# A convolution block on one core: the ternary weights' pieces halved in width and given two buffers, the second weights' extremes moved into the main loop, zeros stored ahead of the weights

## Chip, core and metric

The kernel runs on one core of one Trainium2 chip. The metric is the device time of one execution in microseconds. Before the change three runs took 2253.93, 2255.93 and 2258.55 us; their median, 2255.93 us, is the time before.

## What is computed

The input is `x` of shape (8, 256, 56, 56) in fp32. Two layers follow each other, each with a skip connection.

```
# layer 0: an involution of the group-normed input
g = groupnorm(x, 32 groups)
ker = w_span @ (w_reduce @ g + b_reduce) + b_span        # 16 groups of 7*7 weights for each pixel
x = x + sum over the 7*7 neighbours of ker * neighbour(g)

# layer 1: two 3*3 convolutions with ternary weights
def ternary(w):                       # over the whole tensor (256, 256, 3, 3)
    tw = w - mean(w)
    mx, mn = max(tw), min(tw)
    lo, hi = mn + (mx - mn) / 3, mx - (mx - mn) / 3
    return where(tw < lo, -1, where(tw > hi, 1, 0))
def conv(v, w): return conv3x3(v, ternary(w)) + centre tap once more
o1 = relu(batchnorm(conv(groupnorm(x), w1)))
o2 = batchnorm(conv(o1, w2))
x = x + relu(o1 + o2)
```

The change concerns the weights `w1` and `w2` of layer 1. Each has 256 x 256 x 9 numbers, held as 128 partitions of 4608. To make a weight ternary, the kernel first needs its mean, its largest and its smallest element, then one pass over it with the two thresholds. That pass also forms six "planes" from the three taps of each filter row (sums and differences of the taps), since the convolution is done in a Winograd manner over the rows. The planes go to a DRAM scratch tensor `wqd`, from which the convolution stage loads them much later.

## The kernel before

Four stages follow each other. The start loads the first image, takes its group-norm statistics, and makes the first of the matrices described next. The main loop does layer 0. Then come the two convolutions, and a last stage that adds everything up and stores the output.

**Main loop.** An image is cut into four quarters of 64 channels (the two halves of the picture fill the 128 partitions). A quarter is worked in ten rows of tiles, so there are 8 x 4 x 10 = 320 rows. For each quarter a matrix `a` is made from the reduced image `kr` in 14 units (`generate`, line 761). In a unit, TensorE writes `pg` (line 782), and ScalarE (line 786) and VectorE (line 791) move it with its bias into `a`. TensorE's `pg` has two PSUM buffers, so a unit waits until the one before the last is emptied. A row (`apply_row`, line 801) multiplies `a` with `q`, the patches of the input: four sevenths of a `q` come by DMA from the DRAM scratch `xtd` (line 742), the rest from TensorE transposes of `xe` (line 749, copied at 752). Its result `pa` goes through ScalarE (`inv`, line 827) and VectorE (line 828) to GpSimd (called POOL in the profile), which adds it to `x` (line 831). The rows of a quarter interleave with the units of the next quarter, and with the statistics, the group-norm parameters and the reductions `pk` (line 651) of the next image.

`xtd` is filled by `prep` (line 695): POOL writes a normed strip into the single buffer `xn` (line 674), TensorE transposes it (line 717), ScalarE copies it out (line 720), SP stores it (line 708). The borders of `xtd` must be zero. They are stored once in the start, at line 637, as sixteen DMAs whose source is `xn`, which then still holds zeros. POOL therefore cannot write its first strip before these sixteen have landed.

**Order of the work.** Almost all DMAs are issued by SP, one after the other as the text has them; an issue waits for its data, for its target buffer, and for one of eight semaphores to come free from an earlier DMA. Some stores are put into a list `tasks` and issued by `transfer`, two at the start of each row. Within a row the tile framework's order is the order of the text; `pin` (line 864) ties the last instruction of each row to the first of the next on every engine.

**Extremes, before.** Line 627 takes the buffer `wf` and the four DMAs of line 631 fill it with all of `w1` and `w2`, ahead of the zeros. `extremes` (line 195) is a generator: six times a maximum and a minimum on VectorE (lines 208 and 209, 768 elements each) and a sum on ScalarE (line 210); then the partial results are joined, TensorE sums and transposes them across partitions (lines 222, 223 and 230), and some tiny VectorE instructions give the mean and the two thresholds. Line 900 chains the twelve steps of both weights and then both endings; three steps are taken after each third of the first image's reduction (line 906), the others one after each unit of the first matrix (line 914).

**Pieces, before.** `quantize` (line 248) makes a weight ternary in 16 pieces of 96 output columns (`QN`), 288 elements a partition. A piece has one buffer, `piece`. Line 257 loads it; then, a yield apart, come lines 261 and 262 (two comparisons), 264 to 277, 279 to 281, 283 and 284. The store (line 287, six planes of 96 columns) is put into `tasks`. One piece takes seven rows, and the next piece begins when the store has been issued. Both weights' pieces run one after the other from row 8 on (`QUANT_AT`): 32 pieces in 224 rows, some five and a half images; line 984 takes one step at the end of each row.

Of the kernel before, what the change touches and what calls it, by code (L numbers as in the profile page):

```python
# [2 lines left out]

# [5 lines left out]
F32 = mybir.dt.float32  # L9
F32R = mybir.dt.float32r  # L10
AF = mybir.ActivationFunctionType
ALU = mybir.AluOpType
# [5 lines left out]
P = 128  # L18
B, C, H, W = 8, 256, 56, 56
HW = H * W  # L20
CT = C // P
# [37 lines left out]
A_COLS = (NT * NP + NE * PX) * GQ  # L59
# [19 lines left out]

QN, QJ = 96, 3 * C // 96
QS = WT
SLOT = (0, 2, 3, 4, 5, 1)
QM = 6


@with_exitstack
def involution_tri_block_kernel(
# [3 lines left out]
    nc = tc.nc  # L93
# [11 lines left out]
    wq_d = [dram.tile([P, QS * CT * 3 * C], F32, tag=f"wqd{i}", name=f"wqd{i}") for i in range(2)]  # L105
# [84 lines left out]
        return sc, bi  # L190

    def piece_of(pool, name):
        return pool.tile([P, (4 + QS) * QN], F32, tag="piece", name=f"piece_{name}")

    def extremes(w, cols, pool, transposer, psum_tile, name):
# [8 lines left out]
        s, mx, mn = col(QM), col(QM), col(QM)  # L204
        f = nf // QM
        for j in range(QM):
            v = w[:, j * f:(j + 1) * f]
            nc.vector.tensor_reduce(mx[:, j:j + 1], v, AX.X, ALU.max)
            nc.vector.tensor_reduce(mn[:, j:j + 1], v, AX.X, ALU.min)
            nc.scalar.activation(v, v, AF.Identity, accum_out=s[:, j:j + 1])  # L210
            yield
        sums, ends = col(), col(2)
        nc.vector.tensor_reduce(sums, s, AX.X, ALU.add)
        nc.vector.tensor_reduce(ends[:, 0:1], mx, AX.X, ALU.max)
        nc.vector.tensor_reduce(ends[:, 1:2], mn, AX.X, ALU.min)
        nc.vector.tensor_scalar(ends[:, 1:2], ends[:, 1:2], -1.0, None, ALU.mult)
        v = piece_of(pool, name)
        nc.vector.memset(v[:, :P], 1.0)
        yield

        ps = psum_tile(f"ends_{name}")
        nc.tensor.matmul(ps[:, P:P + 1], v[:, :P], sums, start=True, stop=True)
        nc.tensor.transpose(ps[:2, :P], ends, transposer)
        mean, top = cols[:, 0:1], col()
# [3 lines left out]
        yield  # L228
        ps = psum_tile(f"all_{name}")
        nc.tensor.transpose(ps[:, :2], v[:2, P:2 * P], transposer[:2, :2])  # L230
        ex = col(2)
# [6 lines left out]
        d, q0, r, th = (col() for _ in range(4))  # L238
# [9 lines left out]
    def quantize(dst, w_dram, cols, pool, tasks, name):  # L248


        mean, lo, hi = (cols[:, k:k + 1] for k in range(3))
        for t in range(CT):
            for j in range(QJ):
                v = piece_of(pool, name)
                w, u = v[:, :3 * QN], v[:, 3 * QN:]
                o = (t * QJ + j) * 3 * QN
                nc.sync.dma_start(w, w_dram[:, o:o + 3 * QN])
                yield
                yield
                g = u[:, :3 * QN]  # L260
                nc.vector.tensor_scalar(g, w, mean, hi, ALU.subtract, ALU.is_gt)
                nc.vector.tensor_scalar(w, w, mean, lo, ALU.subtract, ALU.is_lt)
                yield
                nc.vector.tensor_tensor(g, g, w, ALU.subtract)

                def part(x, k):
                    return x[:, k * QN:(k + 1) * QN]


                c0, c1 = max(C, j * QN) - j * QN, min(2 * C, (j + 1) * QN) - j * QN  # L270
                if c0 < c1:
                    g1 = part(u, 0)[:, c0:c1]
                    nc.vector.tensor_scalar(g1, g1, 2.0, None, ALU.mult)

                e, f = part(w, 0), part(w, 1)
                g1, g0, g2 = (part(u, k) for k in range(3))
                nc.vector.tensor_tensor(e, g0, g2, ALU.add)
                yield
                nc.vector.scalar_tensor_tensor(f, g2, 4.0, g0, ALU.mult, ALU.add)
                nc.vector.tensor_tensor(part(u, 3), e, g1, ALU.add)  # L280
                nc.vector.tensor_tensor(part(u, 4), e, g1, ALU.subtract)
                yield
                nc.vector.scalar_tensor_tensor(part(u, 5), g1, 2.0, f, ALU.mult, ALU.add)
                nc.vector.scalar_tensor_tensor(part(u, 6), g1, -2.0, f, ALU.mult, ALU.add)

                def store(u=u[:, QN:], o=t * 3 * C + j * QN):
                    nc.sync.dma_start(
                        bass.AP(dst[:].tensor, dst[:].offset + o,
                                [[QS * CT * 3 * C, P], [CT * 3 * C, QS], [1, QN]]), u)

                tasks.append(store)
                yield
                yield

    def weights(i, k):

# [221 lines left out]
    with ExitStack() as ph1:  # L518
# [19 lines left out]
        apool1 = ph1.enter_context(tc.tile_pool(name="apool1", bufs=1))  # L538
# [71 lines left out]
        ident_sb = fixed([P, P], "ident_sb", ident)  # L610
# [11 lines left out]
        xe = [fixed([P, NX, HQ, QX], f"xe{i}") for i in range(2)]  # L622
        for v in xe:
            nc.gpsimd.memset(v, 0.0)

        nf = CT * 9 * C
        wf = apool1.tile([P, A_COLS], F32, tag="a1", name="wf")
        for i, v in enumerate((w1, w2)):
            for j in range(2):
                o = j * nf // 2  # L630
                nc.sync.dma_start(wf[:, i * nf + o:i * nf + o + nf // 2], v[:, o:o + nf // 2])
        zero = xn.rearrange("p k r x -> p (k r x)")

        for d in (d for ds in xt_d for d in ds):
            for r0, n in ((0, PAD), (PAD + HH, HQ - PAD - HH)):
                e = n * QX * RP // P
                nc.sync.dma_start(
                    bass.AP(d[:].tensor, d[:].offset + r0 * QX * RP, [[e, P], [1, e]]), zero[:, :e])

        def reduce(b, py):  # L640

# [254 lines left out]
        thresholds = [pieces.tile([P, 32], F32, tag=f"cols{i}", name=f"cols{i}") for i in range(2)]  # L896
        ext = [extremes(wf[:, i * nf:(i + 1) * nf], thresholds[i], pieces, ident_sb, ps_one, f"w{i}")
               for i in range(2)]
# [34 lines left out]
        for k in rows[:QLEAD]:  # L933
            transpose_q(*k)
        pin()
        norm = iter(())
        quant = chain(*(quantize(wq_d[i], v, thresholds[i], pieces, tasks, f"w{i + 1}")
                        for i, v in enumerate((w1, w2))))
        last = None
        for m, (b, c) in enumerate(quarters):  # L940
            a = a_next
# [6 lines left out]
            for ty in range(TY):  # L948
                r = c * TY + ty
# [91 lines left out]
    with ExitStack() as ph4:  # L1041
# [95 lines left out]
```

## Time and profile before

| | |
|---|---|
| median of three runs | 2255.93 us |
| the profiled execution | 2269.48 us |
| its span, first to last instruction | 2267.7 us |
| mean granted TensorE clock | 0.924 |
| first `pk` matmul, first `pg`, first whole row (`pa`) | 24.4, 47.3, 80.7 us |
| end of the main loop, first convolution matmul | 1148, 1156 us |
| second convolution, last stage | 1600.7, about 2021 us |
| TensorE (PE) busy | 1866.4 us, 82% |
| VectorE (DVE) busy | 1706.7 us, 75% |
| ScalarE (ACT) busy | 1268.3 us, 56% |
| DMA of the piece stores | 32 of 288 KB, in runs of 384 B |

The profile is of one execution. A row for a group of instructions names its line, engine, operation and tile ("out<-in"), the shape, and how often it came. A wait's row reads: the engine, tile and line that waited, what released it, microseconds in total, times, longest. A window's row gives, for a stretch of time, the busy time of each engine and the number of instructions in brackets, then the granted TensorE clock, the share of the DMA engines that was busy, and GB/s.

### The profile page before, as it was taken

To read this page: it belongs to the slowest core of one execution; us is meant where nothing else is said; L and a number is where in the kernel's file an instruction comes from. 1 tells how busy PE (TensorE), PEld (TensorE's weight loads), DVE (VectorE), ACT (ScalarE), POOL (GpSimd) and SP (SyncE) were. 2 spreads that over 40 slices of the span, in tenths; PEclk is the share of its full clock that TensorE was granted. 3 is DMA by queue.
4 is the path that set the end of the run, shared out by engine and by line. 5 is a ranking of instruction groups with operands and counts; after the bars stand their busy time and mean duration, and the time that the engine had idled before them with its cause. 6 is when DMAs were issued, how large, how long until landed. Compare 5 with 4: busy or idle time off the path is not lost.

```text
span 2267.7 us, 72706 instructions
## 1 busy us (share of the span) xinstructions
PE 1866.4 (82%) x31088; PEld 1716.6 (76%) x31088; DVE 1706.7 (75%) x2906; ACT 1268.3 (56%) x2461; POOL 584.5 (26%) x1320
## 2 busy tenths in 40 slices
PE   4889899898998989999879999999799999970000
PEld 3778777777877877778779999999799999970000
DVE  6676857667585775655689999998999999975444
ACT  3555455455554645556446766665576666673434
POOL 2545546364563645546400000000000000000000
PEclk9899999999999999999989999999899999995555
DMA  6556646566474754645453333334333333369999
GB/s 211 154 157 181 199 131 206 147 192 189 131 221 120 225 164 138 197 119 160 138 206 116 129 134 140 119 116 161 133 138 117 116 116 116 116 255 401 410 430 403
DMA packets 156447, 411.24 MB, mean 181 GB/s; under 512 B 51550, under 2 KB 62172, under 8 KB 148444
## 3 DMA queue, kind: packets, MB, share of 16 engines
q1 hardware_dynamic: 150528, 376.56, 49.9%
q10 hardware_dynamic: 5596, 30.03, 3.2%
q8 instruction: 245, 4.01, 0.8%
q14 instruction: 78, 0.64, 0.1%
HBM read 264.05 MB, written 142.48 MB: 179 GB/s over the span
## 4 chain that ended last, share of the span: by engine, by line
PE 38%; DMA 7%; DVE 3%; ACT 1%; issue 1%; ACTq 0%; SPq 0%; POOL 0%; DVEq 0%
PE c L464 37%; DMA y1f<-y1d 3%; DMA x1f<-x1d 2%; DMA out_y<-x1f 1%; DVE x1f L1064 1%; DMA y2f<-y2d 1%; ACT dummy L416 1%; DVE y1f L1062 0%; ACT y1f L1061 0%; ACT y1f L1063 0%; PE pa L815 0%; PE ptq L749 0%; DVE q L346 0%; DVE r L366 0%; DVE u L373 0%
## 5 line engine op out<-in xcount | busy, mean ns | idle before, releaser
L464 PE MATMUL c<-pl,wq 128*128 128x392 f32 x4608 | 857.1, 348 | 20.2 <-ACT pl L351 20.2
L464 PEld LDWEIGHTS c<-pl,wq 128*128 128x128 f32 x4608 | 855.1, 189 | 22.0 <-ACT pl L351 20.7
L791 DVE TENSOR_TENSOR a<-pg,bt 126x756 f32<-126x756 f32 (+3 forms) x640 | 393.2, 656 | 192.7 <-ACT a L786 147.3
L782 PE MATMUL pg<-kr,wl 64*126 64x140 f32 (+1 forms) x6144 | 459.4, 294 | 14.3 <-DVE a L791 7.1
L782 PEld LDWEIGHTS pg<-kr,wl 64*126 64x126 f32 x6144 | 396.8, 196 | 66.4 <-issue 41.5
L815 PE MATMUL pa<-a,q 126*32 126x48 f32 x17920 | 273.2, 208 | 62.3 <-issue 38.5
L815 PEld LDWEIGHTS pa<-a,q 126*32 126x32 f32 x17920 | 223.1, 111 | 115.8 <-issue 53.4
L786 ACT ACTIVATE a<-pg,bt 126x126 f32<-126x126 f32 x768 | 243.3, 475 | 102.6 <-PE pg L782 102.4
L831 POOL TENSOR_TENSOR x<-x,inv 128x168 f32<-128x168 f32 x320 | 166.4, 520 | 438.5 <-DVE inv L828 375.5
L828 DVE SCALAR_TENSOR_TENSOR inv<-pa,half_sb,inv 128x168 f32<-128x168 f32 x320 | 117.1, 366 | 171.0 <-ACT inv L827 144.8
L351 ACT CAST pl<-r 128x812 fp32r<-128x812 f32 x192 | 162.5, 868 | 145.2 <-DVE r L346 126.9
L752 ACT COPY q<-ptq 126x384 f32<-126x384 f32 x320 | 138.2, 481 | 162.7 <-issue 96.2
L331 POOL MEMSET xp<- 128x116 f32 x32 | 6.3, 195 | 829.4 <-DVE a L346 829.4
L416 ACT ACTIVATE dummy<-y,nc 128x1568 f32<-128x1568 f32 (+2 forms) x144 | 210.1, 1459 | 5.3 <-DVE y L484 3.5
L674 POOL TENSOR_SCALAR xn<-x,gn 128x224 f32<-128x224 f32 (+2 forms) x384 | 179.1, 486 | 130.0 <-PE pt L717 70.8
L352 DVE TENSOR_TENSOR pl<-r,pl 128x812 fp32r<-128x812 f32 x192 | 187.2, 1002 | 28.2 <-ACT pl L351 27.0
L674 POOL TENSOR_SCALAR xe<-x,gn 128x168 f32<-128x168 f32 (+2 forms) x384 | 161.2, 439 | 0.0
L720 ACT COPY stg<-pt 98x512 f32<-98x512 f32 x128 | 74.9, 585 | 137.0 <-issue 88.5
L749 PE MATMUL ptq<-ident_sb,xe 128*126 128x128 f32 x960 | 144.2, 285 | 4.6 <-DVE var_a L170 2.6
L150 DVE BATCH_NORM_STATS2 st<-x 128x6 f32<-128x392 f32 x256 | 138.3, 557 | 11.8 <-DMA x<-in_x 10.2
L827 ACT ACTIVATE inv<-pa,half_sb 128x168 f32<-128x168 f32 x320 | 128.2, 401 | 26.8 <-PE pa L815 25.7
L1011 ACT ACTIVATE xp<-raw,gn 128x392 f32<-128x392 f32 (+1 forms) x124 | 82.6, 721 | 62.9 <-DVE a L346 58.9
(144 smaller groups left out, 1846.2 us busy)
## 6 DMA issues: line engine op xcount, KB each, us to landing
q<-xtd SPq DMA_DIRECT2D x320, 252.0 KB
raw<-x1d SPq DMA_DIRECT2D x32, 812.0 KB
raw<-y1d SPq DMA_DIRECT2D x32, 812.0 KB
x<-in_x SPq DMA_DIRECT2D x64, 392.0 KB
xtd<-stg SPq DMA_DIRECT2D x128, 196.0 KB
x1d<-x SPq DMA_DIRECT2D x64, 392.0 KB
y1d<-y SPq DMA_DIRECT2D x30, 784.0 KB
y2d<-y SPq DMA_DIRECT2D x30, 784.0 KB
```

Of the source, the lines that this page charges most:

```text
L150: nc.vector.bn_stats(st[:, j, :], xt[:, j * NC:(j + 1) * NC])
L351: nc.scalar.copy(hi, r)
L352: nc.vector.tensor_tensor(lo, r, hi.bitcast(F32), ALU.subtract)
L416: nc.scalar.activation(dst, v, f, bias=shift[:, to:to + 1], accum_out=stats[:, to, j, n:n + 1])
L464: nc.tensor.matmul(ps[:, to, :NM], wq[k][:, t, dx, to * P:(to + 1) * P], part[:, t, :, dx:dx + W], start=(c == 0), stop=(c == last))
L674: nc.gpsimd.tensor_scalar(dst[:, i - d - k0:f - d - k0, :, x0:x0 + n], v[:, i:f, :, j0:j0 + n], scale, bias, ALU.mult, ALU.add)
L749: nc.tensor.transpose(pt[:NQ, k * P:(k + 1) * P], xe[c % 2][:, k, PY * ty:PY * ty + QY].rearrange("p r x -> p (r x)"), ident_sb)
L782: nc.tensor.matmul(dst, wl[rows, c, gp, o:o + NQ], kr[py][rows, px, :], start=True, stop=True)
L786: nc.scalar.activation(whole[:, g0 + i, p0 + j], ps[:NQ, i, j * nt:(j + 1) * nt], AF.Identity, bias=bt[:, c, g0 + i, p0 + j:p0 + j + 1])
L791: nc.vector.tensor_tensor(dst[:, g0:g0 + 2, p0:p0 + nv].rearrange("q g p t -> q g t p"), ps[:NQ, :, t0 * nv:t1 * nv].rearrange("q i (t p) ...
L815: nc.tensor.matmul(ps[o:o + 32, k * 2 * n:(k + 1) * 2 * n], q[:NQ, k, o:o + 32], av[:, t + k, g * 2 * n:(g + 1) * 2 * n], start=True, stop ...
L831: nc.gpsimd.tensor_tensor(xv, xv, iv.rearrange("p t (y x) -> p y t x", x=PX), ALU.add)
```

## The change

There are four edits.

First, a piece has 48 columns and 144 elements a partition, so that there are 32 for each weight, and the piece buffer has two homes of half the size. Two pieces go together in a period of seven rows: the first is loaded in row 0, compared in row 2, turned into planes in row 3 and stored in row 6; the second runs three rows behind. Loads and stores are issued by SP directly in their row, no longer through `tasks`. `paced` takes a table of what is to be done in which row.

Second, `w2` is no longer loaded in the start. Its extremes are found in the main loop, between the pieces of `w1` and those of `w2`, from twelve loads of 384 elements into the piece buffers, two in five rows.

Third, the sixteen stores of zeros come before the load of `w1`, where they came after the loads of both weights.

Fourth, the small columns in which extremes keep their numbers are shared, and only two steps of the extremes are taken after each third of the first reduction.

The host prepares the weights in pieces of `QN` columns, so their layout in DRAM follows. The convolution stages, the last stage and the scratch `wqd` are the same.

```diff
-QN, QJ = 96, 3 * C // 96
+QN, QJ = 48, 3 * C // 48
-QM = 6
+QM, QM2 = 6, 12
...
-        return pool.tile([P, (4 + QS) * QN], F32, tag="piece", name=f"piece_{name}")
+        return pool.tile([P, (4 + QS) * QN], F32, tag="piece", bufs=2, name=f"piece_{name}")
+
+    def paced(events):
+        for r in range(max(events) + 1):
+            for f in events.get(r, ()):
+                f()
+            yield
...
+        def fetch(j):
+            held[j] = piece_of(pool, name)[:, :f]
+            nc.sync.dma_start(held[j], w_dram[:, j * f:(j + 1) * f])
+
+        def seek(j):
+            v = w[:, j * f:(j + 1) * f] if w is not None else held.pop(j)
             nc.vector.tensor_reduce(mx[:, j:j + 1], v, AX.X, ALU.max)
             nc.vector.tensor_reduce(mn[:, j:j + 1], v, AX.X, ALU.min)
             nc.scalar.activation(v, v, AF.Identity, accum_out=s[:, j:j + 1])
-            yield
+        events = {}
+        for j in range(n):
+            if w is not None:
+                events[j] = [lambda j=j: seek(j)]
+            else:
+                r = 5 * (j // 2) + j % 2 * 2
+                events.setdefault(r, []).append(lambda j=j: fetch(j))
+                events.setdefault(r + 3, []).append(lambda j=j: seek(j))
+        yield from paced(events)
...
+        if w is None:
+            yield
...
+        def fetch(k):
+            v = held[k] = piece_of(pool, name)
+            nc.sync.dma_start(v[:, :3 * QN], w_dram[:, k * 3 * QN:(k + 1) * 3 * QN])
...
+        events = {}
+        for k in range(CT * QJ):
+            r = 7 * (k // 2) + k % 2 * 3
+            for n, f in ((0, fetch), (2, ternary), (3, planes_of), (6, store)):
+                events.setdefault(r + n, []).append(lambda f=f, k=k: f(k))
+        yield from paced(events)
...
-        nf = CT * 9 * C
-        wf = apool1.tile([P, A_COLS], F32, tag="a1", name="wf")
-        for i, v in enumerate((w1, w2)):
-            for j in range(2):
-                o = j * nf // 2
-                nc.sync.dma_start(wf[:, i * nf + o:i * nf + o + nf // 2], v[:, o:o + nf // 2])
         zero = xn.rearrange("p k r x -> p (k r x)")
 
         for d in (d for ds in xt_d for d in ds):
...
+        nf = CT * 9 * C
+        wf = apool1.tile([P, A_COLS], F32, tag="a1", name="wf")
+        for j in range(2):
+            o = j * nf // 2
+            nc.sync.dma_start(wf[:, o:o + nf // 2], w1[:, o:o + nf // 2])
...
-        found = chain(*(islice(v, QM) for v in ext), *ext)
+        found = ext[0]
...
-            for _ in range(3):
+            for _ in range(2):
                 next(found)
...
-        quant = chain(*(quantize(wq_d[i], v, thresholds[i], pieces, tasks, f"w{i + 1}")
-                        for i, v in enumerate((w1, w2))))
+        made = [quantize(wq_d[i], v, thresholds[i], pieces, f"w{i + 1}")
+                for i, v in enumerate((w1, w2))]
+        quant = chain(made[0], ext[1], made[1])
```

`ternary` and `planes_of` hold the VectorE instructions of lines 261 to 277 and 279 to 284 in their old order; `store` is line 287 with 48 columns.

More of the change, by code (lines that the diff above doesn't have):

```diff
@@ L1 @@
 from contextlib import ExitStack
-from itertools import chain, islice
+from itertools import chain
 import concourse.bass as bass
@@ L192, in piece_of, with extremes @@
     def piece_of(pool, name):
-        return pool.tile([P, (4 + QS) * QN], F32, tag="piece", name=f"piece_{name}")
-    def extremes(w, cols, pool, transposer, psum_tile, name):
+        return pool.tile([P, (4 + QS) * QN], F32, tag="piece", bufs=2, name=f"piece_{name}")
[4 more added lines that the diff above has]
+            yield
+    def extremes(w, w_dram, cols, pool, transposer, psum_tile, name):
         nf = CT * 9 * C
@@ L202, in col @@
             return cols[:, n_cols[0] - n:n_cols[0]]
[L204 to L207, printed above, removed]
+        n = QM if w is not None else QM2
+        s, mx, mn = col(n), col(n), col(n)
+        f = nf // n
+        held = {}
+        def fetch(j):
[3 more added lines that the diff above has]
+            v = w[:, j * f:(j + 1) * f] if w is not None else held.pop(j)
             nc.vector.tensor_reduce(mx[:, j:j + 1], v, AX.X, ALU.max)
@@ L223, in extremes @@
         nc.tensor.transpose(ps[:2, :P], ends, transposer)
-        mean, top = cols[:, 0:1], col()
+        mean, top = cols[:, 0:1], mx[:, 0:1]
         nc.vector.tensor_scalar(mean, ps[:, P:P + 1], 1.0 / (P * nf), None, ALU.mult)
@@ L228, in extremes @@
         yield
+        if w is None:
+            yield
         ps = psum_tile(f"all_{name}")
         nc.tensor.transpose(ps[:, :2], v[:2, P:2 * P], transposer[:2, :2])
-        ex = col(2)
+        ex = mn[:, 0:2]
         nc.vector.tensor_copy(ex, ps[:, :2])
@@ L236, in extremes @@
         nc.vector.tensor_scalar(amn, amn, -1.0, mean, ALU.mult, ALU.subtract)
-        d, q0, r, th = (col() for _ in range(4))
+        d, q0, r, th = (s[:, k:k + 1] for k in range(4))
         nc.vector.tensor_tensor(d, amx, amn, ALU.subtract)
@@ L246, in extremes, with quantize @@
         yield
-    def quantize(dst, w_dram, cols, pool, tasks, name):
+    def quantize(dst, w_dram, cols, pool, name):
         mean, lo, hi = (cols[:, k:k + 1] for k in range(3))
[L252 to L293, printed above, removed]
@@ new lines, in quantize, with part, ternary @@
+        held = {}
+        def part(x, k):
+            return x[:, k * QN:(k + 1) * QN]
+        def fetch(k):
+            v = held[k] = piece_of(pool, name)
+            nc.sync.dma_start(v[:, :3 * QN], w_dram[:, k * 3 * QN:(k + 1) * 3 * QN])
+        def ternary(k):
+            w, u = held[k][:, :3 * QN], held[k][:, 3 * QN:]
+            g = u[:, :3 * QN]
+            nc.vector.tensor_scalar(g, w, mean, hi, ALU.subtract, ALU.is_gt)
+            nc.vector.tensor_scalar(w, w, mean, lo, ALU.subtract, ALU.is_lt)
+            nc.vector.tensor_tensor(g, g, w, ALU.subtract)
+            j = k % QJ
+            c0, c1 = max(C, j * QN) - j * QN, min(2 * C, (j + 1) * QN) - j * QN
+            if c0 < c1:
+                g1 = part(u, 0)[:, c0:c1]
+                nc.vector.tensor_scalar(g1, g1, 2.0, None, ALU.mult)
+            nc.vector.tensor_tensor(part(w, 0), part(u, 1), part(u, 2), ALU.add)
@@ new lines, in planes_of @@
+        def planes_of(k):
+            w, u = held[k][:, :3 * QN], held[k][:, 3 * QN:]
+            e, f = part(w, 0), part(w, 1)
+            g1, g0, g2 = (part(u, k) for k in range(3))
+            nc.vector.scalar_tensor_tensor(f, g2, 4.0, g0, ALU.mult, ALU.add)
+            nc.vector.tensor_tensor(part(u, 3), e, g1, ALU.add)
+            nc.vector.tensor_tensor(part(u, 4), e, g1, ALU.subtract)
+            nc.vector.scalar_tensor_tensor(part(u, 5), g1, 2.0, f, ALU.mult, ALU.add)
+            nc.vector.scalar_tensor_tensor(part(u, 6), g1, -2.0, f, ALU.mult, ALU.add)
@@ new lines, in store @@
+        def store(k):
+            o = k // QJ * 3 * C + k % QJ * QN
+            nc.sync.dma_start(
+                bass.AP(dst[:].tensor, dst[:].offset + o,
+                        [[QS * CT * 3 * C, P], [CT * 3 * C, QS], [1, QN]]),
+                held.pop(k)[:, 4 * QN:])
+        events = {}
[3 more added lines that the diff above has]
+                events.setdefault(r + n, []).append(lambda f=f, k=k: f(k))
@@ L895, in involution_tri_block_kernel @@
         a_next = matrices(0)
-        thresholds = [pieces.tile([P, 32], F32, tag=f"cols{i}", name=f"cols{i}") for i in range(2)]
-        ext = [extremes(wf[:, i * nf:(i + 1) * nf], thresholds[i], pieces, ident_sb, ps_one, f"w{i}")
-               for i in range(2)]
-        found = chain(*(islice(v, QM) for v in ext), *ext)
+        thresholds = [pieces.tile([P, n], F32, tag=f"cols{n}", name=f"cols{n}") for n in (24, 42)]
+        ext = [extremes(wf[:, :nf], w1, thresholds[0], pieces, ident_sb, ps_one, "w0"),
+               extremes(None, w2, thresholds[1], pieces, ident_sb, ps_one, "w1")]
+        found = ext[0]
         for py in range(PY):
```

## Prediction

> **What bounds the kernel now.** I read the busy time by stages first, then the start in order of time, then TensorE's waits, then the main loop image by image, and last the rows of what is edited. The profiled execution took 2269.48 us around a span of 2267.7 us, the runs shown have a median of 2255.93 us: 13.55 us less, 0.6%. I make the sum in the profile's microseconds and take the same difference off the median.
>
> ```profile
> core 0: us, PE busy (x) PEld busy (x) DVE busy (x) ACT busy (x) POOL busy (x), PEclk, DMA share, GB/s
> 24.40:47.30 22.90, 17.17 (x108) 12.82 (x106) 15.76 (x20) 9.70 (x21) 4.01 (x9) 0.85 0.47 164
> 47.30:80.70 33.40, 24.54 (x236) 20.13 (x238) 21.77 (x62) 16.64 (x45) 15.14 (x36) 0.80 0.32 95
> 80.70:1148.00 1067.30, 964.47 (x26120) 825.89 (x26120) 711.52 (x1689) 571.68 (x1563) 555.78 (x1237) 0.97 0.59 169
> ```
>
> Three windows: the first reductions (`pk`), the making of the first matrix (`pg`) up to the first row (`pa`), and the 320 rows. In the rows TensorE is busy 90% of the time; in the two windows before it 74%, at a granted clock of 0.85 and 0.80. The edits reach nothing after 1148 us.
>
> ```profile
> 12.02 5.13 SPq L631 DMA_DIRECT2D wf<-in_w  x4
> 17.27 16.56 SPq L637 DMA_DIRECT2D xtd<-xn  x16
> 35.59 1.34 POOL L674 TENSOR_SCALAR xn<-x,gn 128x224 f32<-128x224 f32 x3 [31.85 <-DMA xtd<-xn]
> 36.98 1.09 PE L717 MATMUL pt<-ident_sb,xn 128*98 128x128 f32 x4 [5.59 <-POOL xn L674]
> 59.83 0.56 PE L222 MATMUL ends_w<-cols,piece_w 128*128 128x1 f32 x2 [3.28 <-DVE piece_w L218]
> 67.74 0.43 PE L222 MATMUL ends_w<-cols,piece_w 128*128 128x1 f32 x2 [1.51 <-DVE piece_w L218]
> ```
>
> The start in order of time, with idle time and releaser in brackets. SP issues four weight loads of 1152 KB, then sixteen stores of zeros that read `xn`. POOL may write `xn` only when these have landed, at 35.59, and TensorE's transpose at L717 stands behind it: 5.59 us idle. The two L222 are TensorE waiting for the extremes of the two weights.
>
> ```profile
> PE pt L717 <- POOL xn L674: 7.6, 4, 5.6
> PE ends_w L222 <- DVE piece_w L218: 4.8, 2, 3.3
> PE pa L815 <- DVE a L791: 1.0, 1, 1.0
> PE pg L782 <- DVE a L791: 1.0, 1, 1.0
> ```
>
> TensorE's waits from 24 to 81 us: 12.4 of the 14.4 us idle concern the zeros and the extremes.
>
> [...] The piece stores go from 384 B runs to 192 B; in the trace's packets 384 B take 22 ns and 256 B 18, so I estimate 16 for 192.
>
> **The change, part by part.**
>
> ```profile
> L261 DVE TENSOR_SCALAR piece_w<-piece_w,cols x32: 414/423/804, 114.2 to 860.5; 128x288 f32<-128x288 f32 x32
> L264 DVE TENSOR_TENSOR piece_w<-piece_w x32: 438/450/784, 117.7 to 867.8; 128x288 f32<-128x288 f32 x32
> L277 DVE TENSOR_TENSOR piece_w<-piece_w x32: 243/255/473, 118.1 to 868.3; 128x96 f32<-128x96 f32 x32
> ```
>
> (min/median/max in ns.)
>
> *Zeros sooner.* In the new order the first store takes the place of the first weight load, at 12.02. The first eight issue as earlier loads give back their semaphores, until about 20; the other eight follow 0.45 us apart (the spacing from 29.96 to 33.38 now), until about 24, and have landed by 26. So POOL begins at about 26, not 35.59. TensorE's `pk` matmuls of the first part end at 31.4 as now, and `xn` is then ready: the 5.59 us go. What is late next is nothing on POOL (24 us free) but the weight load: one tensor of two halves, issued at 24 to 25, each 2.9 us at the 404 GB/s that the window from 20 to 30 us shows: landed by about 29 and 32. VectorE's twelve reductions of 0.956 us then end near 40, ScalarE's six sums near 42, beside `pk`. The two later `pk` parts took 4.95 and 3.67 us; without the wait the clock stays up and both take about 3.8. So `pg` starts near 41.6 where it starts at 47.27: 5.7 us.
>
> *Second weights' extremes out of the start.* From 47.3 to 80.7 go the six reductions and six sums that still stood there, and both waits at L222 (4.8 us): the first weights' extremes are ready about 45, before TensorE asks. The two half-clock stretches (57.7 to 64.5 and 67.9 to 74.8, in the clock records) followed those waits; about 11 us of matmuls lay in them, half of which is clock. Not all comes back, since each `pg` unit also waits for ScalarE and VectorE to empty one of two buffers (a pair of units 4.1 us apart at the end, of which 3.1 is TensorE's). I take 4.8 for the waits and 2.5 of the 5.5 for the clock: 7.3 us. Sum of the start: 5.7 + 7.3 = 13. Bounds: the two kinds of wait (10.4) less a quarter, 8; with all of the clock, 16.
>
> *Pieces of half the columns.* Now one piece has nine VectorE instructions of 2.81 us by the medians and half of one of 0.21, 2.92 in all; the line by line means, contention in, sum to 101.5 us for 32 (1.087 times). Afterwards 64 pieces: two of 144 elements 0.275 each[...], one tensor_tensor 0.300, six of 48 at 0.203, half of one of 0.19: 2.16. Times 64 and 1.087: 150 us. Added: 49 us of VectorE. A row's block grows to 1.0 or 1.2 us from at most 0.85, in four rows of seven as now.
>
> *Extremes in the loop.* 24 reductions of 384 elements[...]: 13.3 us of VectorE; twelve sums of about 0.63 us on ScalarE (7.5 us); twelve loads and four small matmuls. VectorE gains 62 us in the loop in all.
>
> What of that reaches TensorE? Windows cut at the first row of an image:
>
> ```profile
> 629.30:766.10 136.80, 124.10 (x3313) 105.85 (x3312) 94.89 (x229) 73.21 (x201) 71.88 (x160) 0.98 0.62 173
> 766.10:905.40 139.30, 124.48 (x3313) 105.99 (x3312) 93.12 (x226) 73.45 (x201) 71.77 (x160) 0.98 0.60 173
> 905.40:1040.60 135.20, 124.35 (x3312) 106.57 (x3310) 81.95 (x180) 72.97 (x200) 69.95 (x160) 0.96 0.55 156
> ```
>
> The fifth, sixth and seventh image. The seventh has no pieces. The second to sixth average 138.0 us, 2.8 more, with about 13 more of VectorE: at most a fifth of that work reaches the time. Single waits say less: TensorE's waits for VectorE at the turn of a quarter are as long with pieces (0.4 to 1.4 us) as without (0.7 to 1.35), and those that only images with pieces have (at L749, more at L576, five at L782) come to 8 us in all, 8.5% of the work. I take 8.5% of the 62 us, 5; the bounds are 0 and 12.
>
> *Waits added.* ScalarE's sum waits for VectorE's reduction of the same piece; behind it stand `inv` and the copies that TensorE needs. It is two reductions, 1.1 us, in twelve rows. TensorE's L222 and L230 wait for a result made two rows before. Together 1 us; bounds 0 and 4, below nothing excluded as nothing is removed here.
>
> *Stores and loads.*
>
> ```profile
> SPq L742 <- PE pa L815: 419.1, 177, 7.8
> SPq L287 <- DVE st L150: 49.1, 17, 4.4
> SPq L257 <- DMA wqd<-piece_w: 31.1, 20, 3.4
> ```
>
> SP's waits in the rows. The store at L287 now holds SP until VectorE is done (about 103 us with its other lines); three rows later it will not. But SP is idle 419 us for TensorE itself, and a `q` load is issued 10 us or more before its row in nine rows of ten, so I cost the gain at nothing (below: up to 3 us, if a late issue hides in the 38 us of TensorE's waits that the profile calls issue). It gets 74 more DMAs (0.56 us a store, 0.37 a load: 33 us of issue), and 64 landings to wait for, not 32 (31 us more), under the same 419. If that cover were gone, the 31 would count. DMA: 49152 packets of 16 ns for 24576 of 22, over sixteen engines 15 us more in 860, at a share of 0.6: nothing.
>
> Sum: -13 + 5 + 1 = -7 us; 2248.9, said 2249.
>
> **The rivals.**
> *The loop is free.* VectorE has 25% to spare, SP no longer stands; start -13 to -16, loop 0: 2241. For it: no difference at the turns of quarters. Against: it is 80% busy in the first two quarters of an image.
> *The gain is half eaten.* Zeros land later than 26 (two lanes hang on the small loads of ScalarE's queue) or the clock does not come back: -9 at the start; the loop takes a sixth of the 62 us, +9: 2256.
> *Slower: VectorE becomes the bound in the loop.* Blocks of 1.0 to 1.2 us stand before the additions that free TensorE's buffers, and ScalarE waits with them. From 28% of the 62 us passed on it is slower by over 4.5 us (17.5 - 13); at 40%, 25 - 13 = +12: 2268. For it: the first two quarters would be at 85 to 90%. Against: 8.5 to 20% seen.
>
> **How the numbers follow.** Forecast (2249) 0.52; free loop 0.20; half eaten 0.17; slower 0.11. A measurement of this kernel tells apart about 0.2%, 4.5 us: the forecast's lower edge of gain lies close to that. Faster: most of the forecast and all of the free loop, 0.62; same 0.26; slower 0.12. The range reaches from the free loop, start at 16, 2239, to the half eaten gain and a little beyond, 2259.
>
> **What would show it.** POOL's first `xn` near 26 us (over 30: zeros wrong); no wait at L717 over 1 us; first `pg` near 42; no L222 wait over 1 us before the rows, first row near 68; VectorE busy about 1755 us; images two to six near 139 us, the seventh now over 135. SP's wait for VectorE at the piece store gone. Wrong if the rows take over 1080 us from the first `pa`, or the first `pa` comes after 73.

## The result, and the profile after

| | before | after |
|---|---|---|
| median of 7 runs each | 2253.93 us | 2260.50 us |
| lowest and highest | 2248.75, 2258.55 | 2252.03, 2266.53 |
| ratio after to before, 95% interval | | 1.0031 [1.0010, 1.0052] |
| profiled execution (span) | 2269.48 (2267.7) us | 2252.03 (2250.2) us |
| VectorE busy | 1706.7 us | 1746.4 us |
| packets under 512 B | 51550 | 77310 |

The change makes the kernel slower by 0.3%; repeated beside other kernels (e1) it was 1.0045 [1.0030, 1.0060]. The forecast was 2249.0 us and faster. The two profiled executions would have told the opposite, 17.5 us faster: the one of before took 13.55 us more than the median of three runs that the prediction started from, the one of after was the fastest of its seven. One profile of each kernel doesn't settle a difference of this size; the ratios do. In what follows 1% is 22.6 us.

The start, in the windows of the prediction (length, then busy time of PE, PEld, DVE, ACT and POOL with counts, the granted clock, the DMA share, GB/s), cut at first `pk`, first `pg`, first row:

```profile
24.40:39.50 15.10, 15.10 (x108) 11.80 (x109) 10.58 (x15) 7.78 (x16) 4.01 (x9) 1.00 0.51 181
39.50:63.10 23.60, 18.60 (x234) 15.15 (x231) 14.98 (x39) 13.56 (x37) 15.11 (x36) 1.00 0.45 131
63.10:1130.40 1067.30, 956.72 (x26124) 819.45 (x26124) 763.31 (x2028) 574.85 (x1587) 551.01 (x1237) 0.98 0.61 172
```

The first window fell from 22.90 to 15.10 us, the second from 33.40 to 23.60: 17.6 us where 13 were forecast. The clock is 1.00 in both (0.85 and 0.80 before). The timeline shows why the windows are shorter (start, duration, idle and releaser in brackets):

```profile
12.24 11.23 SPq L665 DMA_DIRECT2D xtd<-xn  x16
23.51 0.92 SPq L672 DMA_DIRECT2D wf<-in_w  x2
25.28 1.34 POOL L708 TENSOR_SCALAR xn<-x,gn 128x224 f32<-128x224 f32 x3 [21.53 <-DMA xtd<-xn]
42.49 0.64 PE L751 MATMUL pt<-ident_sb,xn 128*98 128x128 f32 x4 [0.65 <-POOL xn L708]
42.97 0.28 PE L249 MATMUL ends_w<-cols,piece_w 128*128 128x1 f32 x2
```

GpSimd starts at 25.28, not 35.59; TensorE no longer waits at the transpose, and at L249 (L222 before) stands no wait. TensorE's waits up to the first row (total, times, longest):

```profile
PE pg L816 <- DVE a L825: 2.2, 3, 1.2
PE pt L751 <- POOL xn L708: 1.7, 3, 0.7
PE pa L849 <- DVE a L825: 1.0, 1, 1.0
```

So 12.4 us of waits became 1.7. What took this back lies in the rows. The third, fourth, fifth and seventh image of after:

```profile
335.30:470.50 135.20, 122.43 (x3312) 104.89 (x3310) 103.80 (x293) 73.34 (x200) 71.40 (x160) 0.99 0.64 178
470.50:619.50 149.00, 124.67 (x3317) 106.32 (x3316) 95.76 (x222) 77.51 (x225) 69.98 (x160) 0.97 0.54 162
619.50:753.80 134.30, 122.15 (x3312) 104.52 (x3310) 103.39 (x288) 73.23 (x200) 71.08 (x160) 0.99 0.64 178
894.00:1026.70 132.70, 121.91 (x3313) 104.33 (x3312) 97.40 (x264) 72.95 (x201) 70.96 (x160) 0.99 0.63 178
```

The fourth takes 149 us, 14 more than its neighbours, although VectorE does less in it than in them. (The sixth, not shown, took 140.2, so images of one execution differ by some 6 us without it.) What sets the fourth apart is that the second weights' extremes lie there. TensorE's busy time is 2 us more; the rest is idle: 24.3 us, where the third has 12.8 and the fifth 12.2. Its two longest waits there:

```profile
PE pg L816 <- DVE a L825: 8.9, 6, 1.8
PE br L611 <- ACT q L786: 5.3, 1, 5.3
```

One place of it, in order of time:

```profile
545.70 0.54 DVE L223 TENSOR_REDUCE cols<-piece_w 128x1 f32<-128x384 f32 x1
546.16 0.54 DVE L224 TENSOR_REDUCE cols<-piece_w 128x1 f32<-128x384 f32 x1
546.79 0.52 ACT L225 ACTIVATE piece_w<-piece_w 128x384 f32<-128x384 f32 x1 [4.10 <-DVE cols L224]
547.31 0.84 ACT L786 COPY q<-ptq 126x384 f32<-126x384 f32 x2
547.82 1.02 PE L611 MATMUL br<-gn,wr 64*64 64x1 f32 x16 [5.35 <-ACT q L786]
```

ScalarE stood 4.10 us at the sum, because VectorE had the group norm's small steps and an addition to do before the two reductions. The copy of `ptq`, whose source TensorE had finished at 542.5, stood behind the sum, and TensorE stood 5.35 us behind the copy, at `br`, a small matmul of the next image's group norm, for which it waits 1.6 us in the neighbours.

### The profile page after: what moved, and what is told of

Read it like the earlier page. It is cut to its first block, busy times and chain, and to the rows that moved or that the text cites. A ratio compares the mean times of both kernels' runs of the same rounds, so it can differ in the third digit from the quotient of the medians.

```text
span 2250.2 us, 73180 instructions
## 1 busy us (share of the span) xinstructions
PE 1851.0 (82%) x31088; PEld 1704.6 (76%) x31088; DVE 1746.4 (78%) x3214; ACT 1266.5 (56%) x2473; POOL 579.4 (26%) x1320
## 2 busy tenths in 40 slices
DMA packets 187587, 411.28 MB, mean 183 GB/s; under 512 B 77310, under 2 KB 93564, under 8 KB 179836
## 3 DMA queue, kind: packets, MB, share of 16 engines
q1 hardware_dynamic: 181664, 376.57, 50.8%
## 4 chain that ended last, share of the span: by engine, by line
PE 55%; DVE 7%; DMA 7%; ACT 3%; issue 2%; SPq 0%; POOL 0%; ACTq 0%; DVEq 0%
PE c L499 38%; PE pg L816 7%; PE pa L849 4%; DMA x1f<-x1d 3%; PE ptq L783 2%; DVE a L825 2%; DMA y2f<-y2d 2%; PE pk L685 2%; DMA y1f<-y1d 2%; DVE x1f L1098 1%; ACT a L820 1%; PE pt L751 1%; DVE st L150 1%; ACT dummy L451 1%; DVE inv L862 0%
## 5 line engine op out<-in xcount | busy, mean ns | idle before, releaser
L816 PE MATMUL pg<-kr,wl 64*126 64x140 f32 (+1 forms) x6144 | 449.5, 290 | 32.0 <-DVE a L825 23.0
L816 PEld LDWEIGHTS pg<-kr,wl 64*126 64x126 f32 x6144 | 387.8, 192 | 83.3 <-issue 39.5
L849 PE MATMUL pa<-a,q 126*32 126x48 f32 x17920 | 269.5, 207 | 43.6 <-DVE a L825 21.3
```

The lines of the kernel that those rows point to most:

```text
L816: nc.tensor.matmul(dst, wl[rows, c, gp, o:o + NQ], kr[py][rows, px, :], start=True, stop=True)
L849: nc.tensor.matmul(ps[o:o + 32, k * 2 * n:(k + 1) * 2 * n], q[:NQ, k, o:o + 32], av[:, t + k, g * 2 * n:(g + 1) * 2 * n], start=True, stop ...
```

## The experiments

The theories. A: VectorE's added work in the rows is passed on to TensorE more than at 8.5%. B: the added transfers on SyncE's queue, or their small packets, are not free. C: little is real, and the difference of the profiles is luck. e8 sets two causes for the loss in the fourth image against each other: A1, ScalarE's sum waits in order for VectorE, and A2, the reductions' own time. S, in e9, says that the start's gain reaches the end. In the texts on record images are counted from 0, so the fourth image is "image 3" there. All ratios are against before, taken in the same rounds:

| run | median us | ratio [95%] |
|---|---|---|
| e1, after again | 2266.05 | 1.0045 [1.0030, 1.0060] |
| e2, zeros sooner only | 2255.42 | 0.9993 [0.9976, 1.0010] |
| e3, half pieces only | 2271.30 | 1.0056 [1.0027, 1.0084] |
| e4, after with the old pieces | 2255.73 | 0.9994 [0.9975, 1.0012] |
| e5, e3's loads and stores alone | 2245.21 | 0.9948 [0.9930, 0.9966] |
| e6, e3's VectorE work alone | 2262.48 | 1.0016 [1.0000, 1.0032] |
| e7, no piece work | 2234.43 | 0.9921 [0.9889, 0.9952] |
| e8, after, sum a row later | 2254.85 | 0.9983 [0.9967, 0.9999] |
| e9, start kept, old pieces, sum a row later | 2245.02 | 0.9925 [0.9900, 0.9950] |
| e10, before, VectorE's piece instructions halved | 2270.74 | 1.0031 [1.0013, 1.0050] |
| e11, before, loads and stores halved | 2269.22 | 1.0024 [1.0006, 1.0042] |
| e12, e9 with the ternary step on GpSimd | 2241.92 | 0.9912 [0.9878, 0.9946] |
| e13, e5 with six stores a piece | 2268.76 | 1.0025 [1.0007, 1.0042] |
| e14, e5 with runs of 96 B | 2263.00 | 1.0004 [0.9985, 1.0024] |

The median of before was 2256.36 us beside e1 to e4, 2259.78 beside e5 to e8, 2262.79 beside e9 to e12 and 2261.76 beside e13 and e14.

**e1, after once more.**

> The changed kernel again, for a second profile on the chip of the next three. Theory A (VectorE's added work in the rows is passed on to TensorE): 5 to 9 us slower than before (ratio 1.002 to 1.004), the first row again near 63 us (17 us sooner), and the rows' stretch at least 20 us longer than in a typical execution of the kernel before; the image in which the second weights' extremes lie is 10 us longer than its neighbours. Theory B (SP's queue: twice as many loads and stores hold up the q loads): the same total, but the loss is spread over all images with pieces, and TensorE's waits for q grow. Theory C (the one profile was luck and nothing is lost in the rows): ratio 0.993.

Slower by 0.45%, and its fourth image took 151.1 us beside 137.7 and 136.2, with the same two waits (8.6 and 5.3 us): the place is the same in a second execution. C falls.

**e2, the zeros alone.** Before, with the sixteen stores ahead of all four weight loads:

```
-        for i, v in enumerate((w1, w2)):
-            for j in range(2):
-                o = j * nf // 2
-                nc.sync.dma_start(wf[:, i * nf + o:i * nf + o + nf // 2], v[:, o:o + nf // 2])
         for d in (d for ds in xt_d for d in ds):
...
+        for i, v in enumerate((w1, w2)):
+            for j in range(2):
+                o = j * nf // 2
+                nc.sync.dma_start(wf[:, i * nf + o:i * nf + o + nf // 2], v[:, o:o + nf // 2])
```

> Kernel before with the sixteen stores of zeros ahead of the loads of both weights; nothing else changed. All theories: the wait at the first transpose (5.6 us) goes; what is late next is the weights, whose extremes then end later, so that 3 to 8 us are gained (ratio 0.9965 to 0.999). If it is not faster, the wait was hidden by something else in the start.

The first `pg` came at 42.4 us instead of 47.3, so 4.9 of the forecast 5.7 are seen in the trace (4.3 are left at the first row, 76.4 us); the time fell by 1.6 us [gain of 5.4 to loss of 2.3], which doesn't show the gain apart from none. The profile of this kernel, at a span of 2254.8, is closer to the usual execution than the profiled one of before: its images two to six take 137.5 us on average (134.6 to 142.5), its seventh 130.2.

**e3, the half pieces alone.** Before with `QN` 48, two buffers, and `quantize` as after.

> Kernel before with only the pieces halved, given two homes and loaded and stored on their own rows; start and extremes as before. Theory A with the piece's VectorE work (49 us more) as the loss: 10 to 20 us slower (ratio 1.004 to 1.009). Theory A with the loss in the extremes: 0 to 5 us slower. Theory B: 15 us or more slower. My own prediction's step: 4 us slower.

+12.6 us [6.1, 19.0]. The half pieces cost this much by themselves; the seeks (the search for the second weights' extremes in the rows) are not needed for it.

**e4, after without the half pieces.**

```
-QN, QJ = 48, 3 * C // 48
+QN, QJ = 96, 3 * C // 96
```

with `quantize` of before, and the second weights loaded for their extremes in six pieces of 768 elements, each reduced in two halves.

> The changed kernel with the old pieces of 96 columns (one home, stored through the list of tasks), and the second weights' extremes still in the rows, from loads of 768 elements worked in two halves. Theory A with the loss in the pieces: 10 us or more faster than before (ratio under 0.9955). Theory A with the loss in the extremes, and theory of a sum: start 17 us gained, 10 us lost in one image, so 3 to 8 us faster. Theory B: 10 us or more faster, since SP's queue is the old one but for six loads.

It is 11.6 us below after (+10.2 to -1.4), about what e3 lost. Yet it is only level with before, although its first row starts at 62.9 us, where after has 63.1: most of the start's gain is gone. So there is a second loss besides the half pieces. Its fourth image, where the second weights' extremes are, takes 144.4 us, but the third 133.8, the fifth 138.6 and the sixth 142.3: this trace alone does not place the loss; e8 and e9 do.

**e5, e6, e7: the two halves of the piece work.** e5 and e6 are e3 with one kind of work left out, e7 with both, so their convolutions do not get the ternary weights:

```
e5:  for n, f in ((0, fetch), (6, store)):
e6:  for n, f in ((2, ternary), (3, planes_of)):
e7:  for n, f in ():
```

> The half pieces alone (as in e3), of which only the loads and the stores are left: their 9 or 10 VectorE instructions a piece are left out, so the convolutions read weights that were never made. Theory A (VectorE's work is what the loop pays for): the loop loses the whole price of the pieces, about 6 to 7 us for each of 5.5 images, and the time falls some 35 us below before, to about 2220 us. Theory B (the loads and stores, in number or in packets under 512 bytes, hold up SyncE's queue and the q loads): the time stays with e3, about 2268 us. Split: in between, and the distance to e7 is the transfers' share.

> The counterpart of e5: the half pieces' VectorE instructions on two fixed buffers, without their loads and stores; in place of the made weights six plain copies of the weights for each convolution are written in the same rows. Theory A: as e3, about 2268 us, with images 1 to 5 at 138 to 142 us. Theory B: as e7, about 2220 us.

> No piece work at all in the loop, neither VectorE's nor transfers, apart from the six plain copies for each convolution of e6. Both theories: about 2220 us (images at 130 us throughout, as images 6 of e2 and e3 show), which gives the price of all piece work in the loop. If my forecast's premise holds (the loop passes on at most a fifth of VectorE's piece work), it falls by less than 20 us, to 2240 or so.

The engines' busy line on the page of e6 and then of e7:

```profile
PE 1855.4 (82%) x31088; PEld 1706.6 (76%) x31088; DVE 1745.4 (77%) x3202; ACT 1268.4 (56%) x2461; POOL 579.6 (26%) x1322
```

```profile
PE 1843.9 (83%) x31088; PEld 1698.2 (76%) x31088; DVE 1629.3 (73%) x2602; ACT 1266.3 (57%) x2461; POOL 573.5 (26%) x1322
```

116.1 us of VectorE (DVE) cost 1.0016 - 0.9921 = 0.95%, 21 us: 18% is passed on (12 to 25% with both intervals). The transfers alone, e5 less e7, cost 6 us, and -2 to 14 are possible. Both theories expected e7 near 2220, some 37 us below before; it is 17.8 below [25.1, 10.8], half of that, which is within my forecast's "at most a fifth", at its edge. In its profile images two to six average 132.6 us and the seventh takes 132.2, as they should without pieces. Against e2's 137.5 the pieces of before cost 4.8 us an image, by the medians' 17.8 us over five and a half images 3.2; I had read 2.8 within one execution. At 18% the 39 us of VectorE that e3 adds make 7 of its 12.6 us; the rest is left for the transfers.

**e8, the sum a row later.** After with one edit:

```
             nc.vector.tensor_reduce(mn[:, j:j + 1], v, AX.X, ALU.min)
-            nc.scalar.activation(v, v, AF.Identity, accum_out=s[:, j:j + 1])
...
                 events.setdefault(r + 3, []).append(lambda j=j: seek(j))
+                events.setdefault(r + 4, []).append(lambda j=j: add_up(j))
```

`add_up` is the removed line; the first weights keep it in place.

> After with one edit: ScalarE's sum of each of the twelve pieces of the second weights is issued one row later than VectorE's two reductions of it, so ScalarE doesn't stand behind them in order. Theory A1 (the seeks cost through ScalarE's wait): image 3 falls from 149-151 us to 138-140 us and the time by 8 to 12 us against after, to about 2256 us. Theory A2 (they cost through VectorE's own 1.7 us a row ahead of TensorE's matrices): as after, 2266 us, with image 3 still near 150 us.

ScalarE's waits at the sum in after, then in e8, and e8's fourth image:

```profile
ACT piece_w L225 <- DVE cols L224: 21.3, 10, 4.1
```

```profile
ACT piece_w L230 <- DVE cols L224: 2.8, 2, 2.0
```

```profile
472.10:610.10 138.00, 124.87 (x3316) 106.08 (x3314) 94.26 (x221) 78.52 (x224) 69.86 (x160) 0.98 0.60 175
```

149 us became 138, and the ratio went from 1.0045 to 0.9983: 14 us less, some 5 to either side. TensorE's idle time in this image fell from 24.3 us to 13.1: its wait for VectorE's `a` from 8.9 to 0.4, and that at `br` from 5.3 to 1.6. VectorE itself had stood behind ScalarE's `inv`, 27.0 us in this image of after and 17.2 in e8; as far as these waits tell, that is how ScalarE's delay came round to `a`. The reductions are all still there. A1 holds and A2 falls. The ratio carries this, not the one image: in e8's execution the fifth took 141.5 us, at a clock of 0.95.

**e9, the start alone kept.** After with `quantize`, `QN` and buffer of before, and each sum one row behind its reductions.

> After, but with the pieces of before (96 columns, one home, stored by the helper of before) and with the sums of the second weights' pieces one row behind their reductions. Theory S (the start's gain of 17 us reaches the end, and after lost it again through the half pieces, +12, and ScalarE's wait, +12): 15 to 18 us below before, ratio 0.992 to 0.9935, about 2241 us where before has 2257. Rival (the start's gain is given back in the rows whatever stands there, as e4 with ratio 0.9994 could mean): within 4 us of before.

-16.9 us [-22.6, -11.3], where after gains 17.6 up to the first row (e9's own first row starts at 62.4). As far as this interval tells, what the start gains reaches the end. Apart from the place of the sums, and of half of the reductions, which come one row earlier, e9 is e4: from -1.4 to -16.9 us is 15.5, some 7 to either side, a second measure of the price that e8 gives as 14. This version beats before and after.

**e10 and e11, the halving taken apart.** Both are before with one kind of work cut in two:

```
e10:  for i in range(2):
          nc.vector.tensor_scalar(cut(g, i), cut(w, i), mean, hi, ALU.subtract, ALU.is_gt)
          ...
e11:  for i in range(2):
          nc.sync.dma_start(w[:, i * n:(i + 1) * n], w_dram[:, o + i * n:o + (i + 1) * n])
      ...
      tasks.extend(lambda i=i, store=store: store(i) for i in range(2))
```

> Before with each VectorE instruction of a piece cut in two halves of the columns; loads and stores of before, start of before. VectorE's added time is that of the half pieces, 39 us by the busy times of e3 and before. Theory A (VectorE's work at the rate that e6 and e7 show, 21 us for 116): +7 to +8 us, ratio 1.003. Theory B (number and size of the transfers, or the two homes and the pacing): 0.

> Before with each load and each store of a piece cut in two (stores of 192-byte runs, as after); VectorE's instructions, home and pacing of before. Theory B: most of e3's +12.6 us, ratio 1.004 to 1.0055. Theory A: what e5 less e7 allows, at most +3 us of 6, ratio 1.000 to 1.0015.

+7.0 us [2.9, 11.3] and +5.4 [1.4, 9.5]. VectorE's busy time rose by 30.8 us in e10, so 23% was passed on (9 to 37%). The two sum to 12.4 us, and e3, which does both, has 12.6: two homes and the new pacing need not have a price of their own, though with these intervals a few us either way are not excluded. Both theories have a part.

**e12, the ternary step on GpSimd.** e9 with `nc.vector` turned into `nc.gpsimd` in five lines of `quantize` (the two comparisons, the difference, the doubling, the sum of the outer taps).

> As e9, with four to five of the nine or ten VectorE instructions of each piece (the three of 288 columns, the sum of the outer taps and the doubling) given to GpSimd, which is busy 585 us. Takes about 51 us of 77 from VectorE. Theory A (VectorE's time is what counts, at a fifth): 8 to 10 us below e9. Rival (the rows pay for the wait in the chain of a piece or for GpSimd's strips, which now stand behind the pieces): as e9 or slower.

VectorE fell to 1662.4 us, 44 less than in e9. The ratio to before is the best of all, -19.9 us, but its interval holds e9's: whether the step itself gained is not settled.

**e13 and e14, number or size of the transfers.** Over e5, which does no VectorE work on the pieces:

```
e13:  for m in range(QS):
          nc.sync.dma_start(
              bass.AP(dst[:].tensor, dst[:].offset + o + m * CT * 3 * C,
                      [[QS * CT * 3 * C, P], [1, QN]]),
              held[k][:, (2 + m) * QN:(3 + m) * QN])
e14:  n = QN // 2
      nc.sync.dma_start(
          bass.AP(dst[:].tensor, dst[:].offset + k // 2 * 4 * n * QS + k % 2 * n,
                  [[QS * CT * 3 * C, P], [2 * n, 2 * QS], [1, n]]),
          held.pop(k)[:, 2 * QN:8 * QN])
```

> e5 (loads and stores of the half pieces, no VectorE work on them) with each store issued as six, one for each plane: 320 more transfers on SyncE's queue, packets as in e5 (192-byte runs). If the number of transfers is what costs (64 more cost about 5 us in e11), some 20 us more than e5, ratio 1.003 to 1.006 against before. If the packets are: as e5, ratio 0.994 to 0.996.

> e5 with the same number of transfers, each store in runs of 96 bytes in place of 192 (98304 store packets in place of 49152; the made weights' places in memory are not those that the convolutions want, and nothing is computed on them). If the packets cost: 5 to 12 us more than e5, ratio 0.997 to 1.000 against before. If the number of transfers does: as e5, ratio 0.994 to 0.996.

320 more transfers cost 17 us (ratio 0.9948 to 1.0025), 0.054 us each; 49152 more packets in the same number of transfers cost 13 us (to 1.0004), each some 6 to either side. Both count, so neither expectation is the whole. In e14 the places written in memory differ too; what of the 13 is theirs was not measured. Nor are these rates for all such transfers: at them the 128 transfers and 49152 store packets of e5 would cost 20 us over e7, where 6 were measured, 14 at most. For e13 and e11 the trace shows a way. TensorE's waits for a `q` load in the rows, in e5, e13 and e11 (before has none):

```profile
PE pa L831 <- DMA q<-xtd: 0.7, 1, 0.7
```

```profile
PE pa L832 <- DMA q<-xtd: 8.2, 10, 2.2
```

```profile
PE pa L819 <- DMA q<-xtd: 5.4, 5, 2.0
```

SyncE still waits 282 us for TensorE in e13 (386 in e5), so its queue is not full; but before some rows it is late.

## Why the prediction was wrong, step by step

The sum on record was -13 + 5 + 1 = -7 us. The runs give about -17 + 12.6 + 14 = +10; measured were +7 (1.0031) and +10 (1.0045).

**The start: right in mechanism, too small.** 13 us were forecast (bounds 8 and 16); 17.6 were seen and 16.9 reached the end (e9). The zeros gave about what was forecast (4.9 in the trace of e2); their own terms, the wait of 5.6 us and 1.0 less in the `pk` parts, come to 6.6, not to the 5.7 that I took. The two later `pk` parts took 3.67 us each, 3.8 forecast. The rest of the start's gain, about 13, stands against 7.3 for the second weights, in which I let only 2.5 of 5.5 us of lost clock come back. The granted clock was 1.00 from 24.4 to 63.1.

**"Waits added ... Together 1 us": the step that failed.** It priced ScalarE's wait as the two reductions of the same piece, 1.1 us in twelve rows, and let next to nothing of it through. But ScalarE waited for all that stood ahead of those reductions on VectorE too: the ten waits were 2.1 us on average and 4.1 at the longest. Nor did it stop there: TensorE waited for the copy behind the sum, 5.35 us in one row, and for `a`, whose additions stood on VectorE behind ScalarE's late `inv`. Its price was about 14 us; the bound of 4 was far too low. I had named what stands behind the sum on ScalarE, but not what stands ahead of the reductions on VectorE.

**"Stores and loads ... nothing": wrong by about 5.** The halved transfers cost 5.4 us (e11). The DMA engines' time was well estimated: 50.8% of 2250.2 less 49.9% of 2267.7 is 11.5 us, 15 forecast. SyncE's wait at the piece store went as forecast, from about 103 us to some 25:

```profile
SPq L776 <- PE pa L849: 405.5, 186, 10.7
SPq L289 <- DMA wqd<-piece_w: 100.5, 49, 5.4
SPq L318 <- DVE a L825: 7.4, 13, 1.0
```

But 100.5 us of waits for landings stand in its place. The 405 us of slack for TensorE are a sum over all rows; e13's waits for `q` loads, 8.2 us of its 17, speak for the rows that have none setting the price. In e11 TensorE's new waits for `q` loads, 5.4 us, are as long as the loss. In the profiles of after and e3 it has none, so the way in which the transfers cost there is not shown.

**Pieces on VectorE: size of the term.** The tensor_tensors are as estimated (medians 309 ns for 144 elements and 202 for 48, forecast 300 and 203). The trace of before has 450 ns for 288 elements and 255 for 96, so by its rows 144 elements fewer make 146 ns. The two comparisons are not as estimated: 347 and 355 ns, forecast 275. From 288 to 144 elements the first fell by 76 ns (423 to 347), where I took off 148:

```profile
L294 DVE TENSOR_SCALAR piece_w<-piece_w,cols x64: 336/347/602, 95.6 to 996.9; 128x144 f32<-128x144 f32 x64
L296 DVE TENSOR_TENSOR piece_w<-piece_w x64: 307/309/445, 96.6 to 997.9; 128x144 f32<-128x144 f32 x64
L311 DVE TENSOR_TENSOR piece_w<-piece_w x64: 191/202/331, 99.7 to 1001.1; 128x48 f32<-128x48 f32 x64
```

The 24 reductions of 384 elements took 0.54 us each, 13.0 us together where 13.3 were forecast (0.956 for 768 in before). The durations of the added work sum to 68 us, 62 forecast; VectorE's busy time in the rows, in which overlapping instructions count once, gained 51.8. I took 8.5% as passed on from the waits that I could name and had "at most a fifth" as the bound (2.8 us of 13.2 is 21%, and a difference of means, no bound); e6 and e10 show 18 and 23%. At 18% the 52 us are 9, not 5. Both figures came from one execution that was 13.55 us slow, the fifth from its one image without pieces, which at 135.2 us was 3 above that of e7 and 5 above that of e2. After's seventh, now with pieces and forecast over 135, took 132.7. e7 gives a rate of its own: 17.8 us for the piece work of before, transfers included, in which VectorE has 77 us (1706.7 - 1629.3), so at most 23%.

**The rivals.** "VectorE becomes the bound" foresaw the slower side, from 28% passed on. That the time came out there does not make it right: 18 to 23% were passed on, and about half of the rows' loss came through a second engine's order, in one image, with VectorE less busy there than in its neighbours. "The gain is half eaten" had the loop lose 9 us (a sixth of 62 is 10) of a start of 9; it lost some 27 of a start of 17. The sign of being wrong, rows over 1080 us, did not show; they took 1067.3 in the profiled execution. The same length as in the profiled execution of before hid the loss, since that one was slow: e2's rows took 1057.2 (76.4 to 1133.6), those of e1 1077.7.

## What to carry to other kernels

ScalarE, which feeds TensorE, waited for VectorE's result in the row where that is made, and so for the work ahead of it on VectorE, 21.3 us in ten waits; one row later it waited 2.8 us, and the kernel took about 14 us less, for one line moved (e8). Look for such a wait first. Idle time summed over a stage is no proof that added work is hidden: about a fifth of VectorE's work came through, though it was busy for only 62% (e7) to 71% (e6) of the rows, and 64 more small transfers cost some 5 us beside 363 us for which their queue waited for TensorE (e11). Measure the price of such side work once by leaving it out, and take no pass-on rate from single images of one execution, where 3 us are within their scatter (piece images of e2 lie between 134.6 and 142.5).

## What the runs showed of the hardware

- One more transfer on SyncE's queue, over those of e5, cost the kernel 0.054 us (e13), a tenth of the 0.55 us that the issue of a piece store takes in after. Cutting packets of 192 B into two of 96 cost 0.26 ns of the kernel's time for each packet more (e14). In all, the packets' time rose there by 15 ns for each packet more (52.9% of 2255.2 us less 51.3% of 2235.1, times 16, over 49152). A packet of 192 B took 15 ns in after and one of 384 B 22 ns in before (medians), so two for one took 8 ns more of a DMA engine.
- GpSimd took 1.33 us for a comparison of 128 x 288 where VectorE took 0.42, but only 0.80 for the subtraction of the same size, where VectorE took 0.45 (e12, before).
- The granted clock stayed at 1.00 through the start of after, where the waits of 5.6 and 3.3 us are gone; in the same two windows of before it was 0.85 and 0.80. In before it fell from 1.00 to 0.50 at 33.81, 57.70 and 67.94 us, for 6.8 us each time: 2.4 us into the wait of 5.59, 1.1 us into the wait of 3.28, and 0.2 us after the end of one of only 1.51. At 0.50 sixteen `pg` matmuls took 2.07 us (from 60.55), at 1.00 they took 1.15 (from 53.19). Whether the waits made the clock fall was not shown.
